# Lists in place of dense chunks in the second pass of a two-layer graph kernel

## The chip, the cores and the metric

The kernel runs on one core of a Trainium2 chip. The metric is the device time of one execution in microseconds (us), lower is better; a kernel's time is the median of its runs. Five engines matter here: PE multiplies matrices, DVE, ACT and POOL compute elementwise, and SP issues loads and stores. ACT and POOL issue transfers too; POOL's are the gathers, in which a list in SBUF names the rows of a table in memory. An engine executes its instructions in their order, and waits at an instruction until its inputs are there and the tile that it writes is free.

## What is computed

There are n = 3327 nodes (padded to 3328 = 26 blocks of 128), a feature matrix x (n x 512) and a sparse adjacency matrix adj (n x n) whose entries get rarer with both node numbers; the first nodes have the most neighbours. Cut to what matters:

```python
# layer 0
h = relu(layernorm(x))
g = relu(adj @ (h @ W1) + b1)                 # 128 features
x1 = x + adj @ (g @ W2) + b2
# layer 1
h = relu(layernorm(x1))
e = where(adj != 0, exp(-leaky_relu(s_left[:, None] + s_right[None, :])), 0)
x_a = (e / (sum(e, 1) + 1e-5)) @ (h @ W_sa)
t = adj @ h
x_b = t @ W_gcnb + b_gcnb
attn_a, attn_b = sigmoid([t, h] @ Wa.T + ba), sigmoid([t, h] @ Wb.T + bb)
out = x1 + sigmoid(attn_a * x_a + attn_b * x_b)
```

`s_left` and `s_right` are two scores of each row of h. The part of an attention logit that comes from the node's own row h (not from t) is called its own logits below.

## The kernel before, in words

The adjacency matrix lies transposed in memory: row j is the source, column i the destination. Products take source rows as the contraction.

**First pass (L539 to L596).** The columns of the transposed matrix are walked in chunks of 512, the last chunk first (`back`), the final chunk being 256 wide. For each chunk PE adds up u^T A over all 26 source blocks (`acc_u`, L568; u = h @ W1), which gives g. Beside it DVE finds, for every source row, which groups of 32 columns are not empty (`most`, L572), and `make_lists` (L433) turns this into lists: for a destination block of 128, which source rows each of its four groups of 32 needs. A *room* is one list of 64 source rows for each group; block i has `rooms[i]` rooms, and for each room two gathers are issued (q = 0, 1) of 128 rows. So a block costs 2 x rooms gathers of its adjacency entries (tile `ae`, 128 bytes a row), and as many of the rows that they multiply. POOL issues them. In the first pass it gathers `ae` (`gather_behind`, L568 on: each one waits for a product of PE).

Blocks in `OWN` have one dense round ahead of their rooms: the 64 source rows that are the destination's own half block. Their columns are loaded by plain transfers on ACT's queue (`load_own`, L196), and `apart` takes these rows out of the lists.

**Second pass (L813 to L855).** adj @ g is made in one of two ways. For `dense_chunks` (columns 0 to 2303: four chunks of 512, one of 256) the adjacency matrix is loaded a second time and multiplied with g, as in the first pass (`acc_g`, L825). For the last two chunks (`LISTED = 2`: blocks 18 to 25) `list_sums` (L767) multiplies the `ae` entries with rows of g that POOL gathered (`gather_g`, L754). These rows lie in a ring of `GR` = 24, six tiles of four rows: the first 24 gathers are issued ahead of the pass, further ones after each block's sum, and a tile is free when the sums have read it. Between them POOL gathers more `ae`.

As chunks become ready, `make_h1` (L639) makes the rows of layer 1 block by block: PE multiplies with W2 (`px`, L663), DVE adds x and takes the layer norm's statistics, ACT applies it (L244), DVE makes two scores (L623), and SP stores the row to `h_rows` (L637). For blocks that are not in `OWN`, and not in `LATE`, DVE makes the own logits here as well (L627 to L634, three instructions of which two are 512 wide). The rows lie in a ring of 12. Beside this, block 0's layer 1 (the hub, node 0's block, whose columns are dense) is summed over all rows: `e_hub` on DVE and ACT, `acc_hub` on PE (L709). Generators (`next_late`, `hubs`, `make_e_hub`) are advanced at fixed places between the products; a scheduler then fixes each engine's order.

**Layer 1 (L903 on).** Blocks are done from 25 down to 1. `attend` (L917) gathers the block's rows of h (2 x rooms gathers of 128 rows of 2,080 bytes, on POOL), or loads its own row for a dense round, and makes e; `sums` (L968) multiplies, four 64 x 64 x 512 products (L981) for each round; `turn`, `weigh` and `finish` transpose, multiply with W_gcnb (L1035) and W_sa (L1042), and write out. `fetch_ae` adds two `ae` gathers for each block until all are in. Every row gather comes after all `h_rows` stores.

The ring and the places of the sums, as the code says them:

```python
GR = 24
SUMS = {1: (14, 16, 18, 20, 24), 2: (16, 18, 20, 22, 25)}   # chunk: after which product
g_tile[0] = l0w.tile([P, D], F32, tag="h", name=f"g_row_{f}", bufs=GR // NU)   # NU = 4
if n in SUMS.get(c, ()):
    next(summing)
elif c and n % 4:
    gather_behind(added)
```

Of the kernel before, what the change touches and what calls it, by code (L numbers as in the profile page):

```python
# [9 lines left out]
F32 = mybir.dt.float32  # L10
# [18 lines left out]
LISTED = 2  # L29
# [9 lines left out]
LATE = 10, 11, 16  # L39

OWN = 1, 6, 7, 8, 12, 13, 14, 15, 17, 18


def list_rooms(n_blocks):

    rooms = [0, 8, 7, 6, 5, 5] + 6 * [4]
    return (rooms + n_blocks * [3])[:n_blocks]
# [3 lines left out]
def kernel(  # L51
# [30 lines left out]
    for k, c in enumerate(dense_chunks):  # L82
        for c0, w in (c, *listed_chunks[k : k + 1]):
            made_order += range(c0 // P, (c0 + w) // P)
# [3 lines left out]
    extra = [int(i in OWN) for i in range(NB)]  # L88
# [29 lines left out]
    bab_row = kept([P, 2], "bab_row")  # L118
    w_own = kept([P, 2, D], "w_own")
# [20 lines left out]
    def segments(i):  # L140

        r = rooms[i] + extra[i]
        n = -(-r // SEG)
        cuts = [-(-r * k // n) for k in range(n + 1)]
        return list(zip(cuts, cuts[1:]))
# [50 lines left out]
    def load_own(i):  # L196

        n = segments(i)[0][1]
        for h in range(2):
            rows = slice(i * P + h * HALF, i * P + (h + 1) * HALF)  # L200
            nc.scalar.dma_start(
                ae[i][h * HALF : (h + 1) * HALF, 0 : n + 1 : n, :GW],
                adjT[rows, rows].rearrange("j (q i) -> j q i", i=GW),
            )
# [54 lines left out]
    with (  # L259
# [35 lines left out]
        def load_weights():  # L295
# [3 lines left out]
            nc.scalar.dma_start(w_own, w_self.partition_broadcast(P))  # L299
            nc.scalar.dma_start(bab_row, b_ab.partition_broadcast(P))  # L300
# [73 lines left out]
        def make_constants():  # L374
# [36 lines left out]
            for r in sorted(set(rooms[1:])):  # L411
                i0, n = rooms.index(r), rooms.count(r)
# [9 lines left out]
                )  # L422
            yield
# [9 lines left out]
        def make_lists(nth, most):  # L433
# [10 lines left out]
            for b in range(w // P):  # L444
                if extra[c0 // P + b]:
                    groups = slice(b * NQ, (b + 1) * NQ)
                    own = flag[:, groups, c0 // P + b]
                    nc.vector.tensor_tensor(own, own, apart, ALU.mult)

# [99 lines left out]
        for n, c in enumerate(back):  # L549
# [37 lines left out]
            with tc.issue_after(chunk_end.ins):  # L587
# [4 lines left out]
                for i in OWN:  # L592
                    if n and c0 <= i * P < c0 + w:
# [32 lines left out]

        def own_logits(i, h, junk):  # L627

            for s in range(2):
                nc.vector.scalar_tensor_tensor(  # L630
                    junk, h[:, :D], 1.0, w_own[:, s, :], op0=ALU.mult, op1=ALU.mult,
                    accum_out=node[i][:, 1 + s : 2 + s],
                )
            nc.vector.tensor_tensor(node[i][:, 1:3], node[i][:, 1:3], bab_row, ALU.add)  # L634
# [4 lines left out]
        def make_h1(c, sT, last):  # L639
# [16 lines left out]
            for b, i in enumerate(blocks):  # L656
# [21 lines left out]
                if not extra[i] and i not in LATE:  # L678
                    own_logits(
                        i, made_row(i),  # L680
                        l0w.tile([P, D], BF16, tag="junk", name=f"junk_{i}", bufs=1),
                    )
# [69 lines left out]
        g_slots, g_rows, g_taken, g_tile = slots(), {}, [], [None]  # L752

        def gather_g(n):  # L754
            for f in g_slots:
# [5 lines left out]
                gather(t, g_dram[:, :], row_h[:, f : f + 1], NP - 1)  # L761
# [5 lines left out]
        def list_sums():  # L767

            for c0, w in listed_chunks:
                acc = bank(psB, f"acc_s_{c0}")  # L770
                for b, i in enumerate(range(c0 // P, (c0 + w) // P)):
                    r = rooms[i] + extra[i]
                    assert fetched[i] == 2 * rooms[i]
                    for k0, k1 in segments(i):
                        for kk in range(k0, k1):
                            for q in range(2):
                                if kk < extra[i]:
                                    t = g[i]
# [21 lines left out]
                late.append(make_h1((c0, w), sT, False))  # L800
# [12 lines left out]
        QUIET = 6  # L813
        SUMS = {1: (14, 16, 18, 20, 24), 2: (16, 18, 20, 22, 25)}
# [3 lines left out]
        for c, (c0, w) in enumerate(dense_chunks):  # L818
            last = c == len(dense_chunks) - 1
            acc = bank(psA, f"acc_g_{c0}")  # L820
            per = CW // w
            for n, j in enumerate(order):
                if n % per == 0:
                    a = load_adj(j, (c0, w), "a2", per)
                added = nc.tensor.matmul(  # L825
# [4 lines left out]
                if n in SUMS.get(c, ()):  # L830
                    next(summing)
                elif c and n % 4:
                    gather_behind(added)
                if n % 2 or (c in (2, 3) and n % 4 == 2):
                    with queued(last_e[0] if last and n < 8 else None):
                        next_late()
                if last and n >= NB - QUIET:
                    continue
                if c > 1 and n % 3 == 2:
                    next(hubs)  # L840
                elif c > 1 and (n > 8 if last else n % 3 == 1):
                    with queued(last_row[0] if last else None):
                        make_e_hub()
# [4 lines left out]
            if last:  # L848
                with queued(last_e[0]):
                    nc.scalar.activation(root, eps, AF.Sqrt)  # L850
                while late:
                    next_late()
            sT = l0w.tile([HID, CW], F32, tag="gT", name=f"sT_{c0}", bufs=3)
            nc.scalar.copy(sT[:, :w], acc[:, :w])
            late.append(make_h1((c0, w), sT, last))  # L855
# [13 lines left out]
    nc.sync.dma_start(bg_row, b_gcnb.partition_broadcast(P))  # L869

# [32 lines left out]
    with tc.tile_pool(name="spw", bufs=2) as spw:  # L903
# [5 lines left out]
        pairs = cycle(rows[1:3] + own + rows[3:] + rows[:1])  # L909
        taken = {}  # L910

        def fetch_ae(n):
            for _ in range(n):
                with queued(gathered[0]):
                    gathered[0] = next(columns, None) or gathered[0]

        def attend(i, seg):  # L917
# [13 lines left out]
            hr = taken[i][k0] = []  # L931
            for k in range(n):
                if k0 + k < extra[i]:
                    h = spw.tile([P, ROW], F32, tag="h_own", name=f"h_own_{i}", bufs=3)
                    nc.sync.dma_start(h, h_dram[i * P : (i + 1) * P, :])
# [28 lines left out]
            elif extra[i]:  # L964
                own_logits(i, hr[0][:, 0, :], spw.tile([P, D], BF16, tag="junk", name=f"junk_{i}"))
# [102 lines left out]

        def own_of(i, inst):

            with queued(inst):
# [250 lines left out]
```

## Time and profile before

| | |
|---|---|
| median of 9 runs (lowest, highest) | 733.28 us (730.62, 737.33) |
| the profiled execution | 731.08 us, span 729.3 us |
| busy: PE, DVE, POOL, ACT | 698.0, 506.8, 465.2, 193.7 us |
| moved | 185.08 MB, 254 GB/s in the mean |
| first pass, to the last `acc_u` | 0 to 215 us |
| second pass with rows and hub sums | 215 to 409 us |
| layer 1, from its first sum | 412.8 to 729.3 us |

A profile is one execution, recorded by the hardware. Its page gives each engine's busy time, the span in 40 slices (a digit is a busy share in tenths), the chain of work that ended last, followed back from the end, and groups of instructions by source line: count, busy time, mean of one, and the idle time before them with what ended it ("releaser"). A float32 product stands as two records, so 52 records are 26 products. A timeline lists an engine's instructions by start and length, equal ones merged, with the idle time before in brackets. Busy times by stretch can be asked for too.

### The profile page before, as it was taken

Reading aid. Unit: us, or ns where it says so; the run is one execution under the profiler, and the core shown is the slowest. Engines: PE = TensorE matmul, PEld = TensorE weight load, DVE = VectorE, ACT = ScalarE, POOL = GpSimd, SP = SyncE. Lnnn points to the kernel's source line nnn. Section 1 sums busy time; section 2 is a strip of 40 time slices with the busy share of each in tenths; the row PEclk is TensorE's granted clock in tenths of the full one; section 3 lists DMA queues with packets and bytes.
Section 4 is the critical chain, followed back from the end, with each engine's and each line's share of the span. In section 5 each row is a group of like instructions: output and inputs, shape, how many; then the busy total and the mean of one; then the engine's idle time right before and its main releaser. Section 6 shows DMA issues by size and latency. Waiting matters only on the chain.

```text
span 729.3 us, 11907 instructions
## 1 busy us (share of the span) xinstructions
PE 698.0 (96%) x3595; PEld 390.4 (54%) x3595; DVE 506.8 (69%) x1625; ACT 193.7 (27%) x402; POOL 465.2 (64%) x490
## 2 busy tenths in 40 slices
PE   8999987999999999898999899999999999999995
PEld 7775433444464344343465456656566665665653
DVE  7778988999994647988987354465656465646452
ACT  6873000000000133335653113123122221312211
POOL 1400476777766777777666777777777777777400
PEclk9999999999999999999999999999999999999998
DMA  8788999999979999989975766678788888888600
GB/s 275 244 268 271 287 319 303 301 308 294 321 211 332 337 305 366 304 292 320 319 253 149 256 174 190 203 214 224 231 264 269 252 245 267 234 259 234 193 30 33
DMA packets 104889, 185.08 MB, mean 254 GB/s; under 512 B 18401, under 2 KB 35441, under 8 KB 104818
## 3 DMA queue, kind: packets, MB, share of 16 engines
q1 hardware_dynamic: 66544, 113.43, 46.9%
q0 software_dynamic: 23264, 57.64, 28.1%
q10 hardware_dynamic: 15010, 13.18, 5.5%
q8 instruction: 30, 0.49, 0.3%
q14 instruction: 41, 0.34, 0.1%
HBM read 162.29 MB, written 22.26 MB: 253 GB/s over the span
## 4 chain that ended last, share of the span: by engine, by line
PE 64%; DMA 12%; DVE 11%; issue 6%; POOL 4%; ACT 2%; SPq 0%; POOLq 0%; DVEq 0%; ACTq 0%
PE acc_u L568 13%; PE acc L981 11%; PE p_b L1035 10%; PE p_a L1042 9%; PE acc_g L825 7%; DMA a<-in_adjT_dram 6%; DMA xb<-in_x_dram 4%; PE pu L333 3%; DVE most L572 3%; PE ptt L995 2%; POOL hr L166 2%; PE pt L325 2%; PE acc_hub L709 1%; DMA hr<-h_rows,row_h 1%; POOL rows L166 1%
## 5 line engine op out<-in xcount | busy, mean ns | idle before, releaser
L166 POOL DMA_INDIRECT ae<-in_adjT_dram,row_a x194 | 202.8, 1045 | 124.0 <-DVE past L519 54.0
L568 PE MATMUL acc_u<-a,rows 128*128 128x512 f32 (+1 forms) x364 | 158.0, 569 | 4.4 <-DMA a<-in_adjT_dram 4.4
L166 POOL DMA_INDIRECT hr<-h_rows,row_h x120 | 124.3, 1036 | 36.8 <-issue 25.3
L572 DVE TENSOR_REDUCE most<-a 128x16 f32<-128x512 f32 (+1 forms) x182 | 112.1, 640 | 11.3 <-DMA a<-in_adjT_dram 10.8
L825 PE MATMUL acc_g<-a,g 128*128 128x512 f32 (+1 forms) x260 | 111.1, 561 | 1.3 <-DMA a<-in_adjT_dram 1.3
L1035 PE MATMUL p_b<-W_g_sb,tyT 128*128 128x257 f32 x416 | 97.1, 385 | 0.8 <-ACT tyT L1008 0.5
L568 PEld LDWEIGHTS acc_u<-a,rows 128*128 128x128 f32 x364 | 64.4, 190 | 62.4 <-issue 44.6
L1042 PE MATMUL p_a<-W_sa_sb,tyT 128*128 128x512 f32 (+2 forms) x216 | 93.5, 576 | 0.0
L1035 PEld LDWEIGHTS p_b<-W_g_sb,tyT 128*128 128x128 f32 x416 | 76.5, 189 | 30.9 <-DVE ae L950 4.9
L166 POOL DMA_INDIRECT rows<-h_rows,row_h x74 | 75.9, 1026 | 25.2 <-issue 12.8
L1010 DVE COPY tyT<-ptt 128x512 f32<-128x512 f32 x51 | 34.8, 686 | 62.6 <-PE ptt L995 62.6
L825 PEld LDWEIGHTS acc_g<-a,g 128*128 128x128 f32 x260 | 48.3, 192 | 49.9 <-issue 40.5
L166 POOL DMA_INDIRECT g_row<-g_rows,row_h x48 | 50.5, 1053 | 18.6 <-issue 12.2
L1042 PEld LDWEIGHTS p_a<-W_sa_sb,tyT 128*128 128x128 f32 x216 | 40.9, 189 | 37.8 <-issue 35.9
L981 PE MATMUL acc<-hr,ae 64*64 64x512 f32 x480 | 57.1, 593 | 0.0
L884 ACT ACTIVATE f<-f 128x2 f32<-128x2 f32 x26 | 5.3, 203 | 157.2 <-DVE f L883 110.0
L343 ACT ACTIVATE gT<-acc_u,b_col 128x512 f32<-128x512 f32 (+1 forms) x7 | 4.6, 657 | 147.3 <-DMA a<-in_adjT_dram 122.0
L623 DVE SCALAR_TENSOR_TENSOR junk<-rows,w_rows 128x512 bf16<-128x512 f32 x52 | 35.8, 688 | 4.6 <-ACT rows L244 3.6
L981 PE MATMUL acc<-rows,ae 64*64 64x512 f32 x296 | 35.1, 592 | 2.8 <-DVE ae L251 2.8
L981 PEld LDWEIGHTS acc<-hr,ae 64*64 64x64 f32 x480 | 25.4, 133 | 19.7 <-issue 19.2
L666 DVE TENSOR_TENSOR xb<-px,xb 128x512 f32<-128x512 f32 x26 | 17.2, 683 | 21.7 <-PE px L663 21.7
L995 PEld LDWEIGHTS ptt<-ident,ty 128*128 128x128 f32 x208 | 24.1, 141 | 14.9 <-issue 12.7
(159 smaller groups left out, 935.2 us busy)
## 6 DMA issues: line engine op xcount, KB each, us to landing
a<-in_adjT_dram SPq DMA_DIRECT2D x286, 256.0 KB
h_rows<-rows SPq DMA_DIRECT2D x26, 260.0 KB
x<-in_x_dram SPq DMA_DIRECT2D x26, 256.0 KB
xb<-in_x_dram SPq DMA_DIRECT2D x26, 256.0 KB
x<-xb ACTq DMA_DIRECT2D x26, 256.0 KB
x1b<-x SPq DMA_DIRECT2D x26, 256.0 KB
out_dram<-va SPq DMA_DIRECT2D x25, 256.0 KB
ae<-in_adjT_dram,row_a POOLq DMA_INDIRECT x194
```

Of the source, the lines that this page charges most:

```text
L166: return nc.gpsimd.indirect_dma_start(out=dst, out_offset=None, in_=table, in_offset=bass.IndirectOffsetOnAxis(ap=rows, axis=0), bounds_ch ...
L333: nc.tensor.matmul(pu[:, :HID], hT[:, k, :], W1_sb[:, k, :], start=(k == 0), stop=(k == KD - 1))
L568: added = nc.tensor.matmul(acc[:, :w], u[j], a[:, :w], start=(j == 0), stop=(j == NB - 1))
L572: nc.vector.tensor_reduce(most[:, : w // GW, j], a[:, :w].rearrange("p (b i) -> p b i", i=GW), axis=AX.X, op=ALU.max, apply_absolute_value ...
L623: return nc.vector.scalar_tensor_tensor(junk, h, 1.0, w_rows[:, s, :], op0=ALU.mult, op1=ALU.mult, accum_out=into)
L666: nc.vector.tensor_tensor(x1, px, x1, ALU.add)
L825: added = nc.tensor.matmul(acc[:, :w], g[j], a[:, n % per, :], start=(n == 0), stop=(n == NB - 1))
L981: added = nc.tensor.matmul(taken[i]["acc"][h][q * HALF : (q + 1) * HALF, :], both[half_p, q * n + k, :], taken[i][k0][k][half_p, q, :D], s ...
L995: moved = nc.tensor.transpose(pt[:, k * P : (k + 1) * P], ty[h][:, k * P : (k + 1) * P], ident)
L1010: last = nc.vector.tensor_copy(dst, src)
L1035: nc.tensor.matmul(p_b[n][:, :WH], tyT[:, k, 0, :], W_g_sb[:, k, n * WH : (n + 1) * WH], start=(k == 0), stop=(k == KD - 1),)
L1042: last = nc.tensor.matmul(p_a[:, c0:c1], tyT[:, k, 1, :], W_sa_sb[:, k, c0:c1], start=(k == 0), stop=(k == KD - 1),)
```

## The change

`LISTED` goes from 2 to 4: sixteen blocks (10 to 25) take their second pass from lists, and only columns 0 to 1279 are loaded twice (chunks of 512, 512 and 256). Nine more blocks (`TOP`) get an own dense round, and a second dense round with the first 64 nodes' rows; their lists leave these rows out (the flag's memset). Rooms are set anew: 97 become 88, dense rounds 10 become 28. A block's rooms and dense rounds together are as many as before, or one more.

After the three dense chunks a loop of 35 steps follows without dense products. It has the list sums at fixed steps (`FREE_SUMS`) and 30 `ae` gathers at others (`FREE_AE`), and advances rows and hub sums; these `ae` gathers are ordered behind the last g gather issued so far. In the third chunk and in this loop a hub sum is advanced only when it is more than five rows behind (`add_behind`). Own logits are made in layer 1 for all blocks, from rows that SP loads again from `h_rows`, and their weights are loaded at the end of layer 0 rather than in the first pass. The first 64 rows of h and of g are loaded once (`h_top`, `g_top`).

```diff
-LISTED = 2
+LISTED = 4
-LATE = 10, 11, 16
-OWN = 1, 6, 7, 8, 12, 13, 14, 15, 17, 18
+TOP = 2, 3, 4, 5, 9, 10, 11, 21, 24
+OWN = TOP + (1, 6, 7, 8, 12, 13, 14, 15, 17, 18)
...
-    rooms = [0, 8, 7, 6, 5, 5] + 6 * [4]
-    return (rooms + n_blocks * [3])[:n_blocks]
+    rooms = [0, 8, 6, 5, 4, 4, 4, 4, 4] + n_blocks * [3]
+    rooms[21] = rooms[24] = 2
+    return rooms[:n_blocks]
...
-    extra = [int(i in OWN) for i in range(NB)]
+    extra = [int(i in OWN) + int(i in TOP) for i in range(NB)]
...
     def load_own(i):
         n = segments(i)[0][1]
-        for h in range(2):
-            rows = slice(i * P + h * HALF, i * P + (h + 1) * HALF)
-            nc.scalar.dma_start(
-                ae[i][h * HALF : (h + 1) * HALF, 0 : n + 1 : n, :GW],
-                adjT[rows, rows].rearrange("j (q i) -> j q i", i=GW),
-            )
+        for k in range(extra[i]):
+            for h in range(2):
+                cols = slice(i * P + h * HALF, i * P + (h + 1) * HALF)
+                rows = slice(0, HALF) if k else cols
+                nc.scalar.dma_start(
+                    ae[i][h * HALF : (h + 1) * HALF, k : k + n + 1 : n, :GW],
+                    adjT[rows, cols].rearrange("j (q i) -> j q i", i=GW),
+                )
...
-            nc.scalar.dma_start(w_own, w_self.partition_broadcast(P))
-            nc.scalar.dma_start(bab_row, b_ab.partition_broadcast(P))
...
+                    if extra[c0 // P + b] > 1:
+                        nc.vector.memset(flag[:HALF, groups, 0:1], 0.0)
...
-                if not extra[i] and i not in LATE:
-                    own_logits(
...
-        QUIET = 6
-        SUMS = {1: (14, 16, 18, 20, 24), 2: (16, 18, 20, 22, 25)}
+        SUMS = 14, 16, 18, 20, 24
+        FREE_SUMS = 4, 5, 6, 7, 8, 18, 19, 20, 21, 22, 30, 31, 32, 33, 34
+        FREE_AE = {8: 6, 22: 6} | {n: 1 + n % 2 for n in range(23, 35)}
+        def add_behind():
+            if len(rows_made) - len(e_added) > 5:
+                next(hubs)
...
-                if n in SUMS.get(c, ()):
+                if c == 1 and n in SUMS:
                     next(summing)
-                elif c and n % 4:
-                    gather_behind(added)
...
+        for n in range(FREE_SUMS[-1] + 1):
+            if n in FREE_SUMS:
+                next(summing)
+            with queued(g_last[0]):
+                for _ in range(FREE_AE.get(n, 0)):
+                    next(columns)
+            next_late()
+            add_behind()
+            make_e_hub()
...
+    w_own = late_w.tile([P, 2, D], F32, tag="w_own", name="w_own")
+    nc.sync.dma_start(w_own, w_self.partition_broadcast(P))
...
+            if k0 == 0:
+                h_own = own_row(i)
             for k in range(n):
                 if k0 + k < extra[i]:
-                    h = spw.tile([P, ROW], F32, tag="h_own", name=f"h_own_{i}", bufs=3)
-                    nc.sync.dma_start(h, h_dram[i * P : (i + 1) * P, :])
+                    h = h_top if k else h_own
                     hr.append(h.unsqueeze(1).to_broadcast([P, 2, ROW]))
...
-            elif extra[i]:
-                own_logits(i, hr[0][:, 0, :], spw.tile([P, D], BF16, tag="junk", name=f"junk_{i}"))
+            else:
+                own_of(i, h_own)
```

## The prediction

> **What bounds the kernel now.** I read the page first, then the stretches by stage, then the chain of work that ended last, and last the timelines of POOL and PE around the two stage borders. The page says that PE is busy 96% of the span, and its chain is mostly PE:
>
> ```profile
> PE   8999987999999999898999899999999999999995
> ...
> PE 64%; DMA 12%; DVE 11%; issue 6%; POOL 4%; ACT 2%; SPq 0%; POOLq 0%; DVEq 0%; ACTq 0%
> ...
> L166 POOL DMA_INDIRECT ae<-in_adjT_dram,row_a x194 | 202.8, 1045 | 124.0 <-DVE past L519 54.0
> ```
>
> The last line is why I don't stop there. POOL issues gathers one after the other. Each takes 1.0 us and is followed by 0.3 us of issue.
>
> The stretches show three limits. The columns are start:end, length, busy time of PE, PEld, DVE, ACT and POOL, granted clock, DMA share, GB/s.
>
> ```profile
> 0.00:217.00 217.00, 207.08 (x1113) 116.93 (x1114) 190.82 (x540) 51.44 (x113) 113.62 (x155) 1.00 0.91 285
> 217.00:272.50 55.50, 54.19 (x252) 23.75 (x251) 29.67 (x97) 8.84 (x19) 39.92 (x39) 1.00 0.97 320
> 272.50:409.00 136.50, 128.83 (x434) 62.34 (x434) 107.64 (x360) 58.50 (x103) 98.99 (x92) 0.99 0.87 291
> 409.00:412.80 3.80, 1.04 (x7) 0.21 (x5) 1.38 (x6) 0.65 (x2) 2.88 (x4) 1.00 0.79 221
> 412.80:700.00 287.20, 286.56 (x1681) 173.56 (x1682) 166.54 (x592) 68.49 (x153) 209.83 (x204) 1.00 0.75 222
> ```
>
> Until 217 runs the first pass, until 409 the second pass with the rows and the hub products, from 412.8 layer 1. Layer 1 is pure PE (0.6 us idle in 287). The second pass is PE and DMA together. The border is a wait for POOL: its timeline has
>
> ```profile
> 252.58 1.23 POOL L166 DMA_INDIRECT g_row<-g_rows,row_h  x1 [0.30 <-issue]
> 254.12 1.16 POOL L166 DMA_INDIRECT ae<-in_adjT_dram,row_a  x1 [0.30 <-PE acc_g L825]
> ...
> 396.84 1.00 POOL L166 DMA_INDIRECT rows<-h_rows,row_h  x1 [2.91 <-DVE e_hub L249]
> ...
> 403.36 1.00 POOL L166 DMA_INDIRECT hr<-h_rows,row_h  x1 [0.30 <-issue]
> ```
>
> The 24 gathers of g end their issue at 254.1, and adjacency gathers follow at once. Layer 1's first row gather starts at 396.84, the sixth at 403.36, and PE's first sum of layer 1 follows at 412.78. PE has hub products until 409, so this border costs it only 2.8 us. So the end is: first row gather + 15.9 us + 316.5 us of PE.
>
> **The change, part by part.** *PE, second pass.* Two chunks of 512 columns go: 52 products of 0.86 us (four of its 520 half records take 1.72 us), 44.6 us. List sums go from 25 rounds to 60 (16 blocks: 46 rooms and 14 dense rounds); three rounds take 0.78 us (258.35 to 259.13), so 35 add 9.1 us. Eight more transposes add 0.9 us. *PE, layer 1.* Rounds are rooms and dense rounds: 107 before, 116 after, each block's count the same or one more. A block of four rounds has a period of 11.67 us (490.66 to 502.33 in the chain), one of three 10.81 us (435.77 to 446.58 on PE's timeline), so nine rounds cost 7.7 us, straight on the path. PE work in all: -44.6 + 9.1 + 0.9 + 7.7 = -26.9 us.
>
> *POOL decides what of this is kept.* In the second pass it issued 48 g gathers and 71 of adjacency. After the change it issues 92 and 30, so 122 in place of 119, and in the changed kernel's order of instructions 24 adjacency gathers stand between the last g gather and the first row gather. Nothing gets shorter there, and the g gathers now come in a ring of 24 rows whose tiles are freed only by list sums on PE. Before, adjacency gathers filled those waits; now nothing stands between:
> - 24 gathers from 221.90 to 254.1, as before (1.342 us each).
> - The next tile is free when block 22's sum has read it. That sum stood at 256.96 to 259.1; restart at 258.6. Stall 4.5 us.
> - 20 gathers until 285.4. The 21st needs rows that block 18's sum reads, and this sum stands on PE behind the third chunk: 272.5 + 4 products with W2 (3.4) + 26 half-wide products of 0.43 (11.2) + 7 hub products (6.0) + 4 transposes (0.5) = 293.6; two more W2 products and the sum itself bring 296.5. Stall 11 us.
> - 78 gathers (48 of g, 30 of adjacency) at 1.303 (quiet) to 1.342 (loaded): 101.6 to 104.7 us. Block 14's sum is needed at 336 and due near 316, so no third stall. First row gather: 398 to 401; I take 400.
>
> *The rows are the other arrival.* The last g gather goes out at 296.5 + 54 x 1.33 = 368 and lands by 371; sum, copies and transposes give 374. PE's order puts rows 16, 17 and 10 to 13 behind this sum. The last two rows took 8 us before (386.45 to 394.5), a row costs DVE 3.8 us (four rows in 365.37 to 383.53, 3.0 us of it idle): 8 + 4 x 3.8 = 23 us, and 3 us to store: 400 as well. The border has no reserve.
>
> *Border.* From the first row gather to the first sum: at least five gathers further (6.5), 3.63 us to land (the shortest row landing on the chain, at 430.65) and 1.85 us of DVE and ACT (410.93 to 412.78), 12.0 us; at most 15.9 as now. The weights that then filled the queues are loaded earlier, so I take 13.5: first sum at 413.5, +0.7.
>
> The Trainium skill's "DMA: Bandwidth & Descriptors" (Anatomy of one DMA — SWDGE path) gives a gather 2.0 us plus bytes/436e3, an estimated 2.6 us for 266 KB. The trace's 3.63 is longer; by the page the border would be 1 us shorter.
>
> *Clock.* Hub products now keep up with the rows. Five are left when the last row is made (397), and with their masks they end near 405, so PE stands still some 8 us before layer 1. In the trace an idle of 2.54 us before 294.58 is followed by this:
>
> ```profile
> 293.00:296.00 3.00, 1.42 (x4) 0.67 (x5) 3.00 (x11) 0.31 (x1) 2.39 (x3) 0.87 0.97 359
> 296.00:299.00 3.00, 3.00 (x5) 1.21 (x4) 3.00 (x12) 1.58 (x2) 2.39 (x3) 0.56 1.02 329
> ```
>
> The clock falls to about half, and six half records took 4.44 us in place of 2.74: +1.7 us. After 2.76 us idle at 410 it did not fall. So 0 to 1.7; I take 1.7.
>
> The skill's "TensorE: Matmul & The Clock Gate" (Part 1: The HAM clock gate) says that an idle window of about 3.4 us halves the clock until PE has been busy as long. It speaks against this change, which trades PE work for PE idle; by it each long gap costs an estimated 1.7 us where PE is the limit.
>
> *Costed at nothing.* Own logits of 13 blocks leave DVE's second pass and join layer 1: 1.54 us each (248.44 to 249.98), 20 us under PE, DVE from 58% to 65%. Without that cover, the six blocks of three rounds would be late by up to 0.3 us each: 0 to 2. Row loads for them: 16 more of 260 KB, against 18 gathers fewer of the same size. Own columns: 36 more loads on ACT's queue, 0.62 us each to issue; the longest run (16, 9.9 us) lies in the 16.96 us for which ACT waits for the last chunk anyway. Their 4,608 pieces of 128 bytes cost at most 43 ns each (that queue's mean: 5.5% of 16 engines over 15,010 packets), 12 us over 16 engines, at least their bytes' 2 us, against 512 KB of weights that leave this stage (1.6 us). I take 0 for the first pass, -2 to +4. List columns fall from 194 to 176: below 1 us.
>
> **Sum.** 729.3 + 0.7 + 7.7 + 1.7 = 739.4 us span, 741.2 with the 1.8 around it. The profiled execution (731.08) is 2.2 under the median 733.28, so as a median 743.4: **743 us, 1.4% slower**.
>
> **Rivals.**
> - *POOL never waits* (faster). If list sums always free tiles in time, the first row gather comes at 221.9 + 122 x 1.303 to 1.342 = 381 to 386, the first sum at 397, and the end at -15.8 + 7.7: 725. It decides when the first row gather is before 389. Against it: the sum of block 18 can't be before 293 by PE's own work. For it: DVE loses 20 us of own logits there, which could pull every row forward.
> - *The rows are late* (slower still). At the old mean pace of 5.9 us a row (26 rows in 240.3 to 394.5) the six last rows end at 374 + 35 + 3 = 412; first sum 425, end +12.2 + 7.7 + 1.7: 755. For it: the border has no reserve, and ACT changes tables twice per pair of rows (1.28 us each).
> - *PE's work is all that counts*: 733.3 - 26.9 = 706. The 128.8 of 136.5 us speak for it, POOL's unchanged count against it.
>
> **Chances.** Forecast 0.68, POOL never waits 0.14, rows late 0.14, PE only 0.04. My low bounds together (first sum 408.5, clock 0, first pass -2) give 734.7, the high ones (rows late, own logits +2) 757. The range 731 to 755 leaves out most of the two fast cases and the far end of the late one. 0.3% (2.2 us) is about what a measurement of this kernel can tell from no change. Faster 0.15 (PE only 0.04, POOL never waits 0.11), within 0.3% 0.09 (its other 0.03, and 0.06 at the forecast's low edge), slower 0.76 (the forecast's 0.62 and the late rows).
>
> **What would show it.** POOL: pauses of 4 to 5 us near 254 and 10 us near 286, the first row gather at 398 to 401, 24 adjacency gathers just before it. PE: third chunk done by 294, idle stretches from 300 on, some 8 us idle before the first layer 1 sum at 413, periods of 10.8 and 11.7 us afterwards. I am wrong if POOL has no pauses, if the first row gather is before 389, or if layer 1 takes less than 322 us from its first sum.

## The result, and the profile after

The changed kernel takes 758.2 us (median of 10 runs, 755.6 to 761.3), the kernel before 733.28: ratio 1.0334, with a 95% interval of 1.031 to 1.0359. Slower, as forecast, but by 25 us instead of 10, and outside the range. The profiled execution has a span of 756.5 us, 17.1 more than the forecast's 739.4. In the runs of own_logits_only and ring_pause_w2 below, and in the first four of ring_pause, the kernel before itself took 829 to 837 us beside them; they are compared with nothing else.

The page of the changed kernel, busy time and the rows by slices:

```profile
PE 698.1 (92%) x3815; PEld 389.7 (52%) x3815; DVE 504.7 (67%) x1637; ACT 192.5 (25%) x399; POOL 475.3 (63%) x507
...
PE   8999979999999999968668599999999999999994
...
PEclk9999999999999999978668799999999999999998
```

PE was to do 26.9 us less work, and is busy as long as before (698.0), in part because it ran at a lower clock: from slice 18 to 23 (321 to 435 us) it is neither full nor at full clock. The stretches show it (columns as in the prediction):

```profile
325.00:400.00 75.00, 52.77 (x269) 22.20 (x270) 37.66 (x123) 26.21 (x45) 57.93 (x57) 0.71 0.45 129
400.00:429.60 29.60, 18.36 (x44) 7.53 (x43) 16.65 (x64) 7.94 (x18) 18.34 (x19) 0.90 0.75 251
429.60:700.00 270.40, 270.00 (x1590) 162.32 (x1590) 169.26 (x599) 63.58 (x137) 210.04 (x199) 0.99 0.74 220
```

In 325 to 400 PE is busy for 52.77 of 75 us at a clock of 0.71, DVE half, and the transfers at 0.45. Only POOL works without a break: 57 gathers of 1.0 us with 0.3 us of issue each fill the 75 us. From 429.6 on PE is full again. POOL's timeline has the border and what leads to it:

```profile
224.99 0.99 POOL L164 DMA_INDIRECT g_row<-g_rows,row_h  x1 [4.88 <-issue]
...
262.81 1.00 POOL L164 DMA_INDIRECT g_row<-g_rows,row_h  x1 [5.62 <-PE acc_s L772]
...
301.49 0.99 POOL L164 DMA_INDIRECT g_row<-g_rows,row_h  x1 [12.27 <-PE acc_s L772]
...
374.12 1.11 POOL L164 DMA_INDIRECT g_row<-g_rows,row_h  x1 [0.30 <-issue]
...
406.24 1.50 POOL L164 DMA_INDIRECT ae<-in_adjT_dram,row_a  x1 [0.30 <-issue]
413.81 0.99 POOL L164 DMA_INDIRECT rows<-h_rows,row_h  x1 [6.08 <-PE acc_hub L697]
```

Both pauses are there. The last line says that the first row gather was not held by POOL, which had been free since 407.7. The releaser named, a hub product, is not the cause either: this gather reads what the `h_rows` stores write, and SP issued the last six of those until 411.0, with weights of layer 1 straight behind them:

```profile
393.91 17.11 SPq L630 DMA_DIRECT2D h_rows<-rows  x6
411.55 0.38 SPq L867 DMA_DIRECT2D W_g_sb<-in_W_gcnb_dram  x1
```

PE's timeline shows why the rows came so late:

```profile
378.51 0.64 PE L772 MATMUL acc_s<-g_row,ae 64*32 64x128 f32 x4 [1.27 <-DMA g_row<-g_rows,row_h]
379.08 2.07 PE L697 MATMUL acc_hub<-rows,e_hub 128*128 128x512 f32 x2
380.95 1.92 PE L697 MATMUL acc_hub<-rows,a_hub 128*128 128x512 f32 x2
382.66 0.42 PE L675 MATMUL pl<-ident,node 128*128 128x128 f32 x1
384.52 0.47 PE L783 MATMUL pt_s<-ident,s 128*128 128x128 f32 x1 [1.45 <-ACT s L780]
384.79 3.14 PE L656 MATMUL px<-W_sb,sT 128*128 128x512 f32 x4
...
388.93 2.84 PE L656 MATMUL px<-W_sb,sT 128*128 128x512 f32 x6 [0.57 <-ACT sT L787]
...
429.66 3.69 PE L1008 MATMUL acc<-rows,ae 64*64 64x512 f32 x16 [9.37 <-DVE ae L251]
```

The last list sum ends at 379.1, the first product with W2 on it starts at 388.93. Between them stand two hub products that take 2 us each (0.86 at full clock), a transpose `pl`, and two older W2 products. ACT's order makes it worse, since the copies of `pl` stand ahead of the copy of the sum, which so starts 4.7 us after the sum's end:

```profile
383.12 0.37 ACT L680 COPY s_left<-pl 64x256 f32<-64x256 f32 x1 [9.02 <-PE pl L675]
...
383.88 0.59 ACT L780 COPY s<-acc_s 128x512 f32<-128x512 f32 x1
```

So there is a chain: g gathers, last sum, six rows, last store, row gathers.

### The profile page after: what moved, and what is told of

It reads as the page before. It is cut to its first block, busy times and chain, and to the rows that moved or that the text cites. A ratio compares the mean times of both kernels' runs of the same rounds, so it can differ in the third digit from the quotient of the medians.

```text
span 756.5 us, 12273 instructions
## 1 busy us (share of the span) xinstructions
PE 698.1 (92%) x3815; PEld 389.7 (52%) x3815; DVE 504.7 (67%) x1637; ACT 192.5 (25%) x399; POOL 475.3 (63%) x507
## 4 chain that ended last, share of the span: by engine, by line
PE 64%; DMA 14%; DVE 9%; issue 7%; POOL 3%; ACT 1%; SPq 0%; POOLq 0%; ACTq 0%; DVEq 0%
PE acc L1008 14%; PE p_b L1062 13%; PE p_a L1069 12%; PE acc_u L570 11%; DMA a<-in_adjT_dram 6%; DMA g_row<-g_rows,row_h 4%; DVE most L574 4%; POOL g_row L164 3%; PE pu L331 3%; PE ptt L1022 3%; PE acc_g L824 3%; PE pt L323 1%; DMA x1b<-x 1%; DMA W_g_sb<-in_w_sum_dram 1%; PE acc_hub L697 1%
## 5 line engine op out<-in xcount | busy, mean ns | idle before, releaser
L164 POOL DMA_INDIRECT ae<-in_adjT_dram,row_a x176 | 179.8, 1022 | 113.8 <-DVE past L521 53.1
L164 POOL DMA_INDIRECT hr<-h_rows,row_h x112 | 118.0, 1053 | 34.1 <-issue 27.7
L164 POOL DMA_INDIRECT g_row<-g_rows,row_h x92 | 97.4, 1059 | 49.9 <-issue 30.2
L574 DVE TENSOR_REDUCE most<-a 128x16 f32<-128x512 f32 (+1 forms) x182 | 113.2, 641 | 13.5 <-DMA a<-in_adjT_dram 12.8
L164 POOL DMA_INDIRECT rows<-h_rows,row_h x64 | 67.6, 1056 | 25.3 <-issue 12.5
L824 PE MATMUL acc_g<-a,g 128*128 128x512 f32 (+1 forms) x156 | 61.1, 530 | 2.1 <-DMA a<-in_adjT_dram 1.9
L1008 PE MATMUL acc<-hr,ae 64*64 64x512 f32 x448 | 54.3, 599 | 0.0
L659 DVE TENSOR_TENSOR xb<-px,xb 128x512 f32<-128x512 f32 x26 | 17.6, 685 | 43.7 <-PE px L656 43.6
L824 PEld LDWEIGHTS acc_g<-a,g 128*128 128x128 f32 x156 | 28.1, 189 | 27.9 <-issue 15.6
L1008 PE MATMUL acc<-rows,ae 64*64 64x512 f32 x256 | 33.0, 620 | 9.4 <-DVE ae L251 9.4
L772 PE MATMUL acc_s<-g_row,ae 64*32 64x128 f32 x368 | 24.4, 294 | 17.1 <-DMA g_row<-g_rows,row_h 16.8
```

What stands on the lines that cost most here:

```text
L164: return nc.gpsimd.indirect_dma_start(out=dst, out_offset=None, in_=table, in_offset=bass.IndirectOffsetOnAxis(ap=rows, axis=0), bounds_ch ...
L574: nc.vector.tensor_reduce(most[:, : w // GW, j], a[:, :w].rearrange("p (b i) -> p b i", i=GW), axis=AX.X, op=ALU.max, apply_absolute_value ...
L772: nc.tensor.matmul(acc[part, b * P : (b + 1) * P], ae[i][half_p, 2 * k0 + q * (k1 - k0) + kk - k0, :GW], t[half_p, :], start=(kk == 0), st ...
L824: nc.tensor.matmul(acc[:, :w], g[j], a[:, n % per, :], start=(n == 0), stop=(n == NB - 1))
L1008: added = nc.tensor.matmul(taken[i]["acc"][h][q * HALF : (q + 1) * HALF, :], both[half_p, q * n + k, :], taken[i][k0][k][half_p, q, :D], s ...
```

## Experiments

Theory: **the rows set the border.** The last g gather, held up by the pauses, fixes the last list sum, and some 35 us later the last row is stored. Rival 1: POOL's count of gathers sets it. Rival 2: the half clock stretches the tail (the time from the end of the last list sum to the first row gather). A number to read in each run is the start of the first row gather (413.81), and what POOL did ahead of it. Experiments 1 to 8 stand beside a kernel before of 732.8 to 733.3 us. A trace is one execution, and executions of one kernel lay several us apart (755.6 to 761.3 for the changed kernel), so a difference of 1 or 2 us between two traces shows little.

**1. Adjacency gathers into the pauses** (ae_in_pauses)

```diff
-        FREE_AE = {8: 6, 22: 6} | {n: 1 + n % 2 for n in range(23, 35)}
+        FREE_AE = {n: 1 + n % 2 for n in range(23, 35)}
...
                 g_rows[f] = t
+                with queued(g_last[0]):
+                    for _ in range({24: 4, 44: 8}.get(len(g_taken), 0)):
+                        g_last[0] = next(columns)
```

> The changed kernel, with 12 of its 30 adjacency gathers moved into POOL's two pauses (4 behind the 24th g gather, 8 behind the 44th). Six of them stood among the g gathers, six among the 24 ahead of the first row gather. Theory (rows): the first row gather waits for the last stored row, which follows the last list sum by some 35 us (379 to 413.8), and this sum follows the last g gather (374.1). Six gathers of 1.3 us leave the g stretch, so the last g gather comes at 366, the first row gather at 406, the span is 749. Rival 1 (POOL's count of gathers sets the border): POOL is free 15.7 us earlier, at 392, and the first row gather follows at 392 to 396, span 735 to 739. Rival 2 (the half clock stretches the tail): the tail keeps its 35 us whatever POOL does, as in the theory.

Measured: 752.08 us, ratio 1.0276 (1.0224 to 1.0329), span 747.6. POOL's timeline:

```profile
393.22 1.00 POOL L164 DMA_INDIRECT ae<-in_adjT_dram,row_a  x1 [0.30 <-issue]
404.70 0.99 POOL L164 DMA_INDIRECT rows<-h_rows,row_h  x1 [10.48 <-ACT s_left L681]
```

POOL was done at 394.2 and stood for 10.5 us. The last g gather came at 367.6, the first row gather at 404.7, each within 2 us of the theory's (366 and 406); rival 1 wanted 396 at the latest.

**2. No adjacency gathers ahead of the border** (no_tail_ae)

```diff
-        FREE_AE = {8: 6, 22: 6} | {n: 1 + n % 2 for n in range(23, 35)}
+        FREE_AE = {8: 6}
```

> The changed kernel, with the 24 adjacency gathers that stand between the last g gather and the first row gather left to layer 1, two for each block. Theory (the last row, not POOL, sets the border): the first row gather stays at 412 to 414 although POOL is idle from 375, and layer 1, where POOL already issues some 1.3 us for each of 200 gathers in 270 us, gets 24 more and becomes longer: 31 us of gathers against some 5 to 10 us of slack, span 770 to 785. Rival (POOL's count sets the border): first row gather at 380 to 400, span under 750. In between: first row gather stays, but layer 1 hides the gathers, span 756.

Measured: 773.95 us, ratio 1.0538 (1.0492 to 1.0584), span 771.9. POOL's timeline again:

```profile
373.72 1.31 POOL L164 DMA_INDIRECT g_row<-g_rows,row_h  x1 [0.30 <-issue]
411.22 1.00 POOL L164 DMA_INDIRECT rows<-h_rows,row_h  x1 [36.18 <-DVE e_hub L249]
```

POOL is idle for 36 us and the row gathers come only 2.6 us earlier: rival 1 is out for this kernel. And the 24 gathers were not free where they went. Layer 1 from its first sum (427.23) takes 344.7 us in place of 326.8; PE is full until 720, and then waits 14.1 us in one piece for the rows of the last blocks, since POOL ends at 743 in place of 714.

**3. A wider ring for the second pause** (adj_ring)

Cut to the new tiles and the call that fills them:

```diff
                 if not k:
-                    g_tile[0] = l0w.tile([P, D], F32, tag="h", name=f"g_row_{f}", bufs=GR // NU)
+                    if GR + 20 <= len(g_taken) < GR + 20 + 32:
+                        g_tile[0] = adjp.tile([P, CW], F32, tag="adj", name=f"g_row_{f}")
+                    else:
+                        g_tile[0] = l0w.tile([P, D], F32, tag="h", name=f"g_row_{f}", bufs=GR // NU)
...
+                if c == 2 and n == NB - 1:
+                    gather_g(34)
```

> The changed kernel, with the g gathers 45 to 76 put into the eight tiles of the adjacency loads, which fall free as the third dense chunk is multiplied; so the second pause (12.3 us) does not wait for the sum of block 18. All 30 adjacency gathers stand behind the last g gather. Theory (rows): the second pause shrinks to at most 3 us and six adjacency gathers leave the g stretch: last g gather at 357, last list sum at 361, first row gather at 395, span 737 to 739. Rival 1 (POOL's count): POOL is free some 10 us earlier, at 397, so first row gather at 397 to 400, span 740 to 743. Rival 2 (the ring does not matter, PE's order does): the list sums stand where they stand on PE and the last sum stays near 379, span 756.

Measured: 740.95 us, ratio 1.0101 (1.0057 to 1.0145), span 740.8: two thirds of the loss gone. The second pause is gone (gathers 44 and 45 follow each other), the last g gather comes at 359.2, the last sum ends at 362.6. The border:

```profile
400.12 1.00 POOL L164 DMA_INDIRECT ae<-in_adjT_dram,row_a  x1 [0.30 <-issue]
401.42 1.00 POOL L164 DMA_INDIRECT rows<-h_rows,row_h  x1 [0.30 <-issue]
```

Here POOL has no idle time ahead of the row gather. The last store was issued at 392.5, so the rows were there near 395, as the theory has it, and now rival 1's bound, 6 us later, decides: its span of 740 to 743 came true, not the theory's 737 to 739. The first pause stayed (6.77 us). First sum at 413.77, 12.35 us after the first row gather.

**4. PE kept busy** (warm), with `WARM` = 4

```diff
                         for kk in range(k0, k1):
+                            if c0 < ND + 2 * CW and kk >= extra[i]:
+                                for _ in range(WARM):
+                                    nc.tensor.matmul(
+                                        warm[:, :P], ident, ident, start=True, stop=True
+                                    )
```

> The changed kernel, with four products of 128 x 128 x 128 without use ahead of each gathered round of the list sums in the last two listed chunks and the one before, so that PE does not stand idle between rounds; they write a bank that nobody reads. Theory (rows wait for gathers): the granted clock of 325 to 400 rises from 0.64 to 0.77 towards 1, the last list sum stays at 379 to 381, and the tail behind it shortens only by the PE work in it, some 2 to 4 us; first row gather at 410 to 413, span 752 to 756. Rival 2 (the half clock is the loss): px and hub products between 379 and 413.8 take half their time, some 8 us less; first row gather at 405, span 747. Third outcome: the added products, some 25 us in all, lie on the path and make the span longer than 757.

Measured: 750.7 us, ratio 1.0249 (1.0204 to 1.0294), span 748.6. With 28 us more of work without use, the kernel ends 7.9 us sooner. The stretch from 325 to 400, and the tail on PE:

```profile
325.00:400.00 75.00, 70.22 (x502) 40.76 (x501) 47.78 (x153) 27.41 (x51) 58.23 (x56) 0.98 0.49 149
```

```profile
376.26 0.42 PE L777 MATMUL acc_s<-g_row,ae 64*32 64x128 f32 x8
376.62 1.13 PE L697 MATMUL acc_hub<-rows,e_hub 128*128 128x512 f32 x2
...
380.81 2.74 PE L656 MATMUL px<-W_sb,sT 128*128 128x512 f32 x6
```

The clock is 0.98 in place of 0.71. From the end of the last sum to the first W2 product on it pass 4.1 us in place of 9.8, at full clock and with `pl` behind the transposes. The last row was stored at 402.5, 8.6 us sooner, and the first row gather at 407.43 follows POOL's last adjacency gather at once. This lies nearer to rival 2 (405, span 747) than to the theory (410 to 413, 752 to 756), so the low clock is a second cause beside the pauses. Its size is not shown by this run alone, since the order changed too: ACT copied the sum at 376.8, 0.1 us after its end. Of the 8.6 us, 0.7 come from an earlier last g gather, 1.7 from a shorter way to the end of the sum, and 5.7 from there to the first W2 product; the other 0.5 lie in the rows. From the rows of the changed kernel, the clock's part of these 5.7 is an estimated 3 us: its two hub products took 3.6 us in place of 1.7, its two older W2 products 3.0 in place of 1.7. The rest is the order. Of the whole, 6.4 us are had before POOL's count binds.

**5. Everything but the longer lists** (listed2). `LISTED = 2` with the old dense loop and its `SUMS`; the new rooms, own columns, first 64 nodes' rounds and own logits stay.

> Everything of the change but the longer lists: LISTED 2 with the dense loop of before, and with the new rooms, own columns, first 64 nodes' rounds and all own logits in layer 1. Theory (each part has its own price): layer 1 from its first sum takes 326 to 327 us in place of 316.5, the first pass loses 2 us, the border stays near its old 412.8; span 740 to 742, so the lists in place of dense chunks cost 15 us of the 27. Rival (the loss is all in the lists): span 729 to 733. Rival (own columns and own logits hurt beyond the rounds): span over 748.

Measured: 744.11 us, ratio 1.016 (1.011 to 1.021), span 742.5, half a us above the theory's. First row gather at 401.1 (396.8 before), first sum at 417.1, layer 1 325.4 us in place of 316.5. So, by difference, 13 of the 27 us come from the rounds, loads and own logits, 14 from the lists.

**6. Own columns loaded later** (late_own). The 28 loads for blocks 1 to 9 leave the first pass and go, one for each step, into the loop after the dense chunks.

```diff
-                    if n and (c0 <= i * P
+                    if n and i * P >= ND and (c0 <= i * P
...
         for n in range(FREE_SUMS[-1] + 1):
+            next(own_later, None)
```

> The changed kernel, with the own-column loads of blocks 1 to 9 (28 of the 56, needed in layer 1 only) taken out of the first pass and issued one for each step of the loop without dense products. Theory (the 128-byte pieces crowd the loads at the end of the first pass): the last acc_u ends at 215 in place of 217, the first g gather starts at 222 in place of 225, and the first dense chunk ends 4 us sooner; all that follows moves with it, span 752 to 753. Rival (the first pass is late for another reason, the list work): first g gather still at 225, span 756; or slower, as ACT issues loads in the tail.

Measured: 762.47 us, ratio 1.0388 (1.0344 to 1.0433), no faster than the change itself. Theory and rival both missed. The last chunk of the first pass took 16.6 us from ACT's previous `gT` to its last, 17.6 in the changed kernel. But the kernel before, which has fewer of these loads, took 17.65, and the seven other runs with all of them 16.75 to 18.5, so no price of the loads can be read from this. And the first chunk ended 6.3 us later (71.67 against 65.33), where no such load is. The waits of the first 50 us show what is new:

```profile
ACT rows L330 <- POOL ae L435: 4.9, 1, 4.9
```

ACT's copy of the first pass now waits once for POOL's clearing of the `ae` tiles: the changed kernel has no such wait in these 50 us, so moving the loads seems to have changed the scheduler's order far from where they were. The price of the own columns in the first pass stays open, and so does the cause of the 3.1 us by which the first g gather was late.

**7. All three together** (combo, and combo2 with late_own on top): wider ring, four adjacency gathers in the first pause, products without use.

> The changed kernel with three of the edits together: g gathers 45 to 76 in the tiles of the adjacency loads, four adjacency gathers in the first pause, and products without use between the gathered rounds. Theory: with the pauses gone and the tail short, POOL's own count is what is left: from 226, 122 gathers of 1.33 us and 2 us of pause, so the first row gather at 390 to 391; the rows are ready at 388 (last sum at 358, tail of 26 us, 3 us to store). 12.4 us to the first sum, 326.8 us of layer 1: span 730, against 729.3 of the kernel before. If the added products delay the list sums by more than they save, the rows are at 396 and the span is 736.

> The kernel of the run combo, with the 28 own-column loads of blocks 1 to 9 issued in the loop without dense products instead of in the first pass. Theory: everything comes 3 to 4 us earlier, first g gather at 222, first row gather at 387, span 726 to 727. If the own-column loads are not what makes the first pass late, as combo.

Measured: 752.27 us (ratio 1.0231, 1.0181 to 1.0281) and 753.42 (1.0272, 1.0226 to 1.0318). Both forecasts missed, by 22 and 25 us of span, and combo's second one, for products that delay the sums (736), by 16. The last g gather came at 359.8 as meant, but the last sum ended at 380.2, 17.6 us later than in adj_ring:

```profile
374.41 1.12 PE L697 MATMUL acc_hub<-rows,a_hub 128*128 128x512 f32 x2
375.46 0.42 PE L784 MATMUL acc_s<-g,ae 64*32 64x128 f32 x8
375.81 1.16 PE L773 MATMUL warm<-ident 128*128 128x128 f32 x8
376.90 0.42 PE L784 MATMUL acc_s<-g_row,ae 64*32 64x128 f32 x8
```

No brackets: PE doesn't wait, and from 325 to the end of the sum it has one wait, of 0.18 us. With the rows of g there in time, the products without use (28.1 us in all) are no longer in the gaps but on the path. The two remedies share one gap, and their gains don't add.

**8. Both pauses filled** (ring_pause): the wider ring of experiment 3, and four adjacency gathers behind the 24th g gather.

> The kernel of the run ring_pause once more: the changed kernel with g gathers 45 to 76 in the tiles of the adjacency loads and four adjacency gathers in the first pause. Theory (POOL's count is the limit that is left): first row gather at 396, against 401.4 in adj_ring, first sum 12.4 us later at 408.5, span 735 to 736. Rival (the rows bind as in the changed kernel): first row gather over 399 with POOL idle ahead of it, then some 16 us to the first sum, span 741.

Measured (ring_pause_e): 739.5 us, ratio 1.008 (1.0052 to 1.0108), span 741.2. The border:

```profile
398.11 1.02 POOL L164 DMA_INDIRECT ae<-in_adjT_dram,row_a  x1 [0.30 <-DVE e_hub L256]
399.43 1.00 POOL L164 DMA_INDIRECT rows<-h_rows,row_h  x1 [0.30 <-issue]
```

POOL never pauses from its first g gather, which came late here (229.08, against 226.46 in adj_ring), to this row gather: 122 gathers in 170.4 us, in adj_ring the same 122 in 175.0. The 4.6 us are the four gathers that now lie in the pause; the theory had 5.4. The late start and the border (14.8 us to the first sum at 414.22) took them back. So the theory's 396 and its span of 735 to 736 were missed. The rival's span came true without its sign, as POOL is not idle ahead of the row gather. The profiled execution was the slowest of the five; the median's span is some 3.5 us shorter, and the interval overlaps that of adj_ring.

What is left against the kernel before can be read from the two traces, 11.9 us in all: the first g gather +7.2, from there to the first row gather -4.6 (174.9 us before, with 119 gathers), the border -1.1, layer 1 +10.5 (327.0 us). So with the pauses gone, this stretch is no longer where time is lost. Layer 1 with its nine rounds and the later first g gather are what remains, and the best version found is 0.8% slower than the kernel before. Why the first g gather is late is open: in the traces of the changed kernel and of the six runs of experiments 1 to 8 that edit nothing of the first pass it came at 224.8 to 229.1.

**9. Without a comparable span** (own_logits_only, ring_pause_w2, and ring_pause four times)

> The changed kernel with both pauses filled and nothing else: g gathers 45 to 76 in the tiles of the adjacency loads, four adjacency gathers in the first pause. Theory (POOL's count is the limit that is left once the pauses are gone): against the run adj_ring, whose first row gather came at 401.4 straight behind POOL's last adjacency gather, four gathers of 1.33 us fewer: 396; the rows are ready at 395. First sum 12.4 us later at 408.5, span 735 to 736. Rival (the rows bind as in the changed kernel): first row gather over 399 with POOL idle ahead of it.

> The kernel of the run ring_pause once more: the changed kernel with g gathers 45 to 76 in the tiles of the adjacency loads and four adjacency gathers in the first pause. Theory (POOL's count is the limit that is left): first row gather at 396, against 401.4 in adj_ring, first sum 12.4 us later at 408.5, span 735 to 736. Rival (the rows bind as in the changed kernel): first row gather over 399 with POOL idle ahead of it, and then some 16 us to the first sum, span 741.

> The kernel of the run ring_pause a third time: the changed kernel with g gathers 45 to 76 in the tiles of the adjacency loads and four adjacency gathers in the first pause. Theory (POOL's count is the limit that is left): first row gather at 396, against 401.4 in adj_ring, first sum 12.4 us later at 408.5, span 735 to 736. Rival (the rows bind as in the changed kernel): first row gather over 399 with POOL idle ahead of it, then some 16 us to the first sum, span 741.

> The kernel of the run ring_pause a fourth time: the changed kernel with g gathers 45 to 76 in the tiles of the adjacency loads and four adjacency gathers in the first pause. Theory (POOL's count is the limit that is left): first row gather at 396, against 401.4 in adj_ring, first sum 12.4 us later at 408.5, span 735 to 736. Rival (the rows bind as in the changed kernel): first row gather over 399 with POOL idle ahead of it, then some 16 us to the first sum, span 741.

> The kernel before with one part of the change alone: all own logits in layer 1, from rows that are loaded again, their weights loaded at the end of layer 0; lists, rooms and own columns as before. Theory (DVE's 1.54 us a block lies under PE in layer 1): layer 1 from its first sum 316.5 to 318.5 us, first row gather within 2 us of 396.8, span 728 to 732, so nothing that can be measured. Rival (the row loads or DVE's later blocks cost): layer 1 over 320 us, and then part of the 8.9 us that layer 1 gained in the run listed2 is not the nine rounds.

> The kernel of the run own_logits_only once more: the kernel before with all own logits in layer 1 and nothing else of the change. Theory (DVE's 1.54 us a block lies under PE in layer 1): layer 1 from its first sum 316.5 to 318.5 us, first row gather within 2 us of 396.8, span 728 to 732. Rival (the row loads or DVE's later blocks cost): layer 1 over 320 us, and then part of the 8.9 us that layer 1 gained in the run listed2 is not the nine rounds.

> The kernel of the run own_logits_only a third time: the kernel before with all own logits in layer 1 and nothing else of the change. Theory (DVE's 1.54 us a block lies under PE in layer 1): layer 1 from its first sum 316.5 to 318.5 us, first row gather within 2 us of 396.8, span 728 to 732. Rival (the row loads or DVE's later blocks cost): layer 1 over 320 us.

> The kernel of the run ring_pause, with two products without use ahead of each gathered round of the last listed chunk only (a few us of PE work, where the run combo had some 25). Theory: the granted clock of 350 to 400 rises and the rows come 2 to 5 us earlier than in ring_pause, but POOL's count still sets the first row gather at 396; layer 1's first sums may run at full clock, 0 to 2 us: span 734 to 736. If it is longer than ring_pause by over 2 us, the products delay the list sums, which is what made combo slow.

> The kernel of the run ring_pause_w2 once more: ring_pause with two products without use ahead of each gathered round of the last listed chunk. Theory: the granted clock of 350 to 400 rises and the rows come 2 to 5 us earlier than in ring_pause, POOL's count sets the first row gather at 396, span 734 to 736. If it is longer than ring_pause by over 2 us, the products delay the list sums, which is what made combo slow.

The kernel before took 829.46, 836.13, 836.27 and 836.84 us beside these runs. own_logits_only had ratios of 0.9942 (0.9906 to 0.9977), 0.9942 (0.9909 to 0.9975) and 0.9915 (0.9877 to 0.9954) to it, so this part alone costs nothing that shows there; its spans can't be set beside 316.5. ring_pause had ratios of 1.0839 to 1.0878 and a median of 902.56 us in its fourth run, ring_pause_w2 1.0839 and 1.0866: no difference between the two shows there, and both lose far more than the 1.008 above. In the fourth trace of ring_pause POOL stood for 62.7 us ahead of the first row gather at 502.72, so there the rows were late again; why is open.

## Why the prediction was right on the direction and wrong on the size

By its own steps, with the 17.1 us of the miss:

- **First pass at nothing** (range -2 to +4): the first g gather came at 224.99, not 221.9: +3.1, inside the range. Its cause is open.
- **Pauses of 4.5 and 11 us:** measured 5.62 and 12.27, which hold 0.3 us of issue each, so +1.7 together. Their place was right, and experiment 3 shows the cause of the second. The gathers took 1.0 us more, mostly late: the 53 steps from the second pause to the last g gather ran 1.37 us each, and I had reckoned 54 of 1.33. Another 0.3 is my rounding of 368.3. The last g gather went out at 374.1 in place of 368: +6.1 with the first pass.
- **"Sum, copies and transposes give 374"** is the step that failed. After the last gather I allowed 3 us to land and 3 us for the sum and all that leads to the first row. It took 5.0 to the end of the sum and 9.8 more: +8.8. I took each operation's own time at full clock with nothing between; PE's order had hub products and older W2 products there, ACT's order the copy of `pl`, and the clock was half. Experiment 4, with full clock and another order, has 4.1 for the 9.8.
- **Six rows 23 us, 3 us to store:** 24.9 us from 388.93 to 413.81, -1.1. The rate of the rows was right. The rival "rows late" came near the time (755 for 758.2) by another mechanism: the rows were not slower, they began later.
- **First row gather at 400 from both sides:** POOL came free at 407.7 and the rows at 413.8. "The border has no reserve" was right, and experiments 1 and 2 show which side holds. "The border is a wait for POOL", my reading of the trace before, was not right: there, too, POOL stood for 2.91 us ahead of its first row gather at 396.84, and SP issued the last stores until 394.2:

```profile
375.55 18.67 SPq L637 DMA_DIRECT2D h_rows<-rows  x5
```

- **Border 13.5:** 15.85 (+2.35). "The weights that then filled the queues are loaded earlier" was wrong: SP issues them at 411.55 to 414.5, straight behind the last store, and so among the row gathers. The kernel before had its first weight load 2.1 us ahead of the first row gather, and a border of 15.9. The border shrinks as the row gathers start later after the first weight load: 15.85 us at 2.3 us after it (changed kernel; the six other traces with 2.2 to 2.3 us have 15.55 to 16.2), 14.8 at 3.2 (ring_pause_e), 14.5 at 4.4 (warm), 12.35 at 8.4 (adj_ring). That the weights are the cause is argued from this order; no run moved them alone, and stores and loads of own rows stand beside them.
- **Clock 0 to 1.7:** priced once, at the border (PE stood for 9.37 us, and the first 16 records took 3.69 us in place of 1.95, so it was right there). I had looked for one long gap; the rows of 325 to 400 show 0.71 for 75 us. This loss sits in the failed step above, an estimated 3 us of its 8.8.
- **Layer 1 +7.7:** 326.8 us from the first sum, with the clock's 1.7 0.9 above the forecast. In experiment 5, 8.9.
- **Own logits at nothing:** experiment 9 speaks for it, though only beside a kernel before of over 829 us.
- **Small slips:** the kernel before has 260 half records of `acc_g`, not 520, and the lowest first sum by the working's own bounds is 410 (398 + 12.0), not 408.5. Neither moves the forecast.

The sum: 13.8 (first row gather: 6.1 + 8.8 - 1.1) + 2.35 + 0.9 = 17.05 us.

## What to carry to other kernels

Work that leaves a full engine is gained only if the chain that then decides gets shorter: walk this chain in the order of every engine that it passes, and charge each thing that stands in the queue between two of its links. PE, once partly idle, was also slower here for what it still had to do (clock 0.71 over 75 us); price that for the whole stretch. Two remedies that fill the same gap are not to be added.

## What the runs showed of the hardware

- The clock falls without one long idle. In stretches of 3 us of the changed kernel:

```profile
322.00:325.00 3.00, 1.15 (x22) 0.61 (x22) 3.00 (x12) 2.49 (x6) 2.39 (x3) 1.00 1.01 318
325.00:328.00 3.00, 1.90 (x16) 0.69 (x16) 0.66 (x4) 0.31 (x1) 2.38 (x3) 0.65 0.80 260
328.00:331.00 3.00, 2.58 (x10) 1.10 (x11) 0.00 (x0) 0.00 (x0) 2.12 (x3) 0.50 0.17 44
```

  PE is busy for 1.15 of 3 us, its longest wait is 1.27 us (before 324.02), and then the clock goes to 0.50. The Trainium skill's "TensorE: Matmul & The Clock Gate" (Part 1: The HAM clock gate) tells of an idle window of about 3.4 us, and in a later paragraph of frequent micro-idles that let the clock swing; here no wait was as long as that window, several short ones sufficed, and the measurement decides. Products without use in these waits held it at 0.98 over the 75 us and, with the order that came with them, made the kernel 7.5 us faster in the median.
- POOL issues a gather each 1.3 us whatever its size (128 rows of 128 bytes or of 2,080 bytes: 1.02 and 1.05 us busy in the mean, and 0.3 of issue), so that the number of gathers is a time of its own: 24 more in layer 1 made it 17.9 us longer, though PE is full until 720.
